# Attention in pairs: both batches of a head group are multiplied with the values in one go, and the turned probabilities go back into the probabilities' buffers

## The chip, the cores and the metric

The kernel runs on one core of a Trainium2 chip. The core has TensorE (PE in the profile: matmuls and transposes), VectorE (DVE), ScalarE (ACT), GpSimd (POOL) and SyncE (SP, which issues the transfers here); they run side by side and wait for each other by semaphores. The metric is the device time of one execution in microseconds (us); a version's time is the median of its runs.

## What is computed

One block of a transformer with cross attention, in float32. The shapes are those of the inputs: `x` and `ctx_2048` are 8 batches of 256 tokens of 512 numbers, 16 heads of 32, and an inner width of 2048. All masks are true.

```python
x = layer_norm(hidden_states, ln1_w, ln1_b)
q = (x @ q_w + q_b).reshape(B, LQ, H, HD).transpose(0, 2, 1, 3)
k = (encoder_hidden_states @ k_w + k_b).reshape(B, LK, H, HD).transpose(0, 2, 1, 3)
v = (encoder_hidden_states @ v_w + v_b).reshape(B, LK, H, HD).transpose(0, 2, 1, 3)
scores = jnp.where(mask, jnp.einsum('bhqd,bhkd->bhqk', q, k) * scale, mask_value)
attn = jax.nn.softmax(scores, axis=-1)
out = jnp.einsum('bhqk,bhkd->bhqd', attn, v)
hidden = out.transpose(0, 2, 1, 3).reshape(B, LQ, D) @ cproj_w + cproj_b + residual
y = jax.nn.gelu(layer_norm(hidden, ln2_w, ln2_b) @ fc_w + fc_b, approximate=True)
return hidden + y @ proj_w + proj_b
```

## The kernel before

**Stages.** The eight batches are four groups of two (`g` from 0 to 3; `GB` is 2). After a prologue that projects keys, queries and values of group 0 comes a long attention stage, up to 347 us of the span, and then a stage for the MLP, which this change does not touch. The projections (`project_qk`, `project_v`, `project_out`) are cut into seven products of quarters, in Strassen's way; each product is 8 or 16 matmuls in the trace and its result is taken out of its PSUM bank by DVE or ACT.

**Units.** Inside the attention stage the work is a list of 32 units `n`: group `g`, head group `hg` (four heads of 32, together 128 partitions) and batch `b` of the group. Units with even `n` have `b` = 0, units with odd `n` have `b` = 1. The main loop (line 1060) has one slot for each unit, and the order in which a slot issues its work is written by hand. On PE a slot is: the scores of unit n + 2 (`scores`, matmuls `s`, four heads side by side in the array, each with 32 rows), the transposes of the probabilities of unit n for heads 0 and 1 (`turn_probs`, tiles `ppt`), a piece or more of a projection for the next group (`between[g, u, 0]`), the transposes for heads 2 and 3, more pieces (`between[g, u, 1]`), and last the product with the values (`attend`, tile `av`, four heads side by side, each with 32 columns). Each engine runs its own instructions strictly in that order.

**The other engines in a slot.** DVE takes the scores out of PSUM (line 664: it adds the mask and finds the row's largest value), ACT takes the exponentials (line 674), DVE the reciprocals of their sums and POOL multiplies (`divide`, line 688); this runs two units ahead of the product with the values. A turned head leaves PSUM as a copy into a tile `pt` (line 702 on DVE for head 0, line 704 on ACT for heads 1 to 3). The result `av` leaves PSUM by an activation on ACT that adds the value bias (line 723).

**Buffers.** The scores of a unit fill four PSUM banks, one for each head, and the pool that holds them (`ps_s`, tag `s`) has just four. So PE can write head j of unit n + 3 only when DVE has read head j of unit n + 2. In slots 0, 1, 5 and 6 of a group the same four banks also hold context or `x` rows that are turned (`turn_ctx`, tiles `pct`; `turn_x`, tiles `pxt`; two of them in one slot), and the scores of the next slot wait until DVE and ACT have taken these out (lines 368 to 379, 415). A second pool of two banks (`ps_t`) is shared by the tiles `ppt` and `av` in turn. In SBUF the probabilities of a unit are one tile `pr` of 16 KB in each partition, with three buffers; the turned copies `pt` have four buffers of 4 KB for each partition, one for each head.

**Work beside it.** `aside[g, u, i]` holds small jobs for POOL, DVE, ACT and SP at four places of a slot: sums of weights and operands, loads and norms.

Of the kernel before, what the change touches and what calls it, by code (L numbers as in the profile page):

```python
# [10 lines left out]
F32 = mybir.dt.float32  # L11
U8 = mybir.dt.uint8
AF = mybir.ActivationFunctionType
# [3 lines left out]
P = 128  # L17
# [5 lines left out]
def tile_xattn_block(  # L23
# [45 lines left out]
    nc = tc.nc  # L69

    B, S, D = x.shape
    SK = enc.shape[1]
    INNER = fc_w.shape[1]
    HD = 32
    GB = 2
# [4 lines left out]
    NQ = S // P  # L80
    NK = SK // P
    NHG = D // P
    HPG = P // HD
    NF = INNER // P
    SCALE = 1.0 / math.sqrt(HD)
    HI, HC, HF, HD2 = INNER // 2, NC // 2, NF // 2, D // 2
# [38 lines left out]
    c_ln1w, c_ln1b, c_qb, c_kb, c_vb, c_ln2w, c_ln2b, c_fcb = col_of  # L125

    def col(base, i):
        return cols[:, base + i : base + i + 1]
# [194 lines left out]
    with ExitStack() as att:  # L323
        work = att.enter_context(tc.tile_pool(name="attwork", bufs=2))
# [3 lines left out]
        ps_t = att.enter_context(tc.tile_pool(name="ps_t", bufs=2, space=PSUM))  # L328
        ps_m = att.enter_context(tc.tile_pool(name="ps_m", bufs=1, space=PSUM))

        mbias, ctxT, xnT, vs, qk, probs, stats, res = ({} for _ in range(8))
        ctxs, xs, att_in, ws, pts = {}, {}, {}, {}, {}
# [71 lines left out]
        def turn_x(g):  # L404
            def piece(c):
                if c == 0:
                    xnT[g] = tokens_operand(work, "xT", f"xnT_{g}")
                ps = turned(f"pxt_{g}_{c}")
                turn(ps, xs[g], c)
                if g == 0 and c % 2:  # L410
                    nc.vector.tensor_scalar(
                        chunk(xnT[g], c), halves(ps), col(c_ln1w, c), col(c_ln1b, c), ALU.mult, ALU.add
                    )
                else:
                    nc.scalar.activation(
                        chunk(xnT[g], c), halves(ps), AF.Identity,
                        bias=col(c_ln1b, c), scale=col(c_ln1w, c),
                    )

            return [lambda c=c: piece(c) for c in range(NC)]  # L420
# [78 lines left out]
        def project_qk(g, tag):  # L499
            w, base = ("k", c_kb) if tag == "kT" else ("q", c_qb)  # L500

            def made(n, bank, u):
                o, k = int(n[0]) - 1, int(n[1]) - 1

                direct = g == 0 and o == 0
                st = None if direct else staged(g, tag, n)
                for i in range(2):
                    b = col(base, 2 * o + i)
                    to = qk[g, i, tag][:, ts(k, S)] if direct else st[:, i, :]
                    if u is None:  # L510
                        nc.scalar.activation(to, bank[:, i, :], AF.Identity, bias=b, scale=1.0)
                    else:
                        nc.vector.scalar_tensor_tensor(
                            to, bank[:, i, :], b, u[:, i, :], ALU.add, ALU.add
                        )
                if not direct:
                    store_quarter(g, tag, o, k, st)

            def src():
                return (ctxT if tag == "kT" else xnT)[g]  # L520

            if g == 0:
                for i in range(2):
                    qk[g, i, tag] = work.tile([P, G], F32, tag=tag, name=f"{tag}_{g}_{i}")
            if g == 0 and tag == "kT":
                return [lambda n=n: eight(f"p{tag}_{g}", n, ws[w], src, made, FIRST_KEYS.get(n, {})) for n in QUARTERS]
            return strassen(f"p{tag}_{g}", lambda: ws[w], src, False, made)
# [38 lines left out]
        def project_v(g):  # L566

            def made(n, bank, u):
                o, k = int(n[0]) - 1, int(n[1]) - 1
                st = staged(g, "v", n)  # L570
                if u is None:
                    nc.scalar.copy(st, bank)
                else:
                    nc.vector.tensor_tensor(st, bank, u, ALU.add)
                store_quarter(g, "v", o, k, st)

            return strassen(f"pv_{g}", lambda: ws["v"], lambda: ctxT[g], True, made)
# [57 lines left out]
        units = [(g, hg, b) for g in range(NG) for hg in range(NHG) for b in range(GB)]  # L635

        def scores(n):

            g, hg, b = units[n]
            qT, kT = qk[g, hg, "qT"], qk[g, hg, "kT"]  # L640
            banks = [
                ps_s.tile([P, NQ, SK], F32, tag="s", name=f"s_{n}_{j}") for j in range(HPG)
            ]
            for i in range(NQ):
                for j in range(HPG):
                    nc.tensor.matmul(  # L646
                        banks[j][:, i, :],
                        qT[j * HD : (j + 1) * HD, b * S + i * P : b * S + (i + 1) * P],
                        kT[j * HD : (j + 1) * HD, b * SK : (b + 1) * SK],
                        start=True,  # L650
                        stop=True,
                    )
            pr = work.tile([P, HPG, NQ, SK], F32, tag="pr", bufs=3, name=f"pr_{n}")
            nmax = small.tile([P, HPG, NQ], F32, tag="nmax", name=f"nmax_{n}")
            sums = small.tile([P, HPG, NQ], F32, tag="sums", name=f"sums_{n}")
            probs[n], stats[n] = pr, (banks, nmax, sums)
# [38 lines left out]
        def turn_probs(n, j):  # L695
            ps = ps_t.tile([P, NK, S], F32, tag="pt", name=f"ppt_{n}_{j}")
            for kc in range(NK):
                for i in range(NQ):
                    nc.tensor.transpose(ps[:, kc, ts(i, P)], probs[n][:, j, i, ts(kc, P)], ident)  # L699
            pt = work.tile([P, NK, S], F32, tag="pt", bufs=4, name=f"pt_{n}_{j}")  # L700
            if j == 0:
                nc.vector.tensor_copy(pt, ps)
            else:
                nc.scalar.copy(pt, ps)  # L704
            pts[n, j] = pt

        def attend(n):

            g, hg, b = units[n]
            if hg == 0 and b == 0:  # L710
                att_in[g] = Att(g)
            av = ps_t.tile([P, S], F32, tag="pt", name=f"av_{n}")
            for kc in range(NK):
                for j in range(HPG):
                    nc.tensor.matmul(  # L715
                        av[j * HD : (j + 1) * HD, :],
                        vs[g, hg][:, b * NK + kc, ts(j, HD)],
                        pts[n, j][:, kc, :],
                        start=(kc == 0),
                        stop=(kc == NK - 1),  # L720
                    )
            x, h, bias = att_in[g], hg % HC, col(c_vb, hg)
            nc.scalar.activation(
                x.t[:, hg, ts(b, S)], av, AF.Identity, bias=bias, scale=1.0
            )

        def sum_att(g, hg, eng=nc.gpsimd):
# [232 lines left out]
        g = 1  # L960
        begin(g, 6, 1, load_res, 0, *QUARTERS)
        begin(g, 7, 1, bias_res, 0)
        g = 2
# [6 lines left out]
        g = NG - 1  # L970
# [24 lines left out]
        def run(pieces):  # L995
            for p in pieces:
                p()
# [25 lines left out]
        k, q, v, tx = project_qk(0, "kT"), project_qk(0, "qT"), project_v(0), turn_x(0)  # L1023
# [19 lines left out]
        nc.gpsimd.tensor_tensor(cbd, cb[:, :S], cb[:, S:], ALU.subtract)  # L1043
        run([q[6], *normalise, v[0]])
        scores(0)
        tx = turn_x(1)
        for j, pieces in enumerate((v[1:2], v[2:3], tx[:2], v[3:4])):
# [12 lines left out]
        for n, (g, hg, b) in enumerate(units):  # L1060
            u = hg * GB + b
            ahead = n + 2 < len(units)
            if ahead:
                scores(n + 2)
                softmax(n + 2, 0)
            run(aside[g, u, 0])
            turn_probs(n, 0)
            turn_probs(n, 1)
            if n + 1 < len(units):
                divide(n + 1)  # L1070
            if ahead:
                softmax(n + 2, 1)
                softmax(n + 2, 2)
            run(between[g, u, 0])
            turn_probs(n, 2)
            turn_probs(n, 3)
            run(aside[g, u, 1])
            if ahead:
                softmax(n + 2, 3)
            run(between[g, u, 1])  # L1080
            run(aside[g, u, 2])
            attend(n)
            run(later)
            later.clear()
            run(aside[g, u, 3])
# [15 lines left out]
    with ExitStack() as mlp:  # L1101
        wpool = mlp.enter_context(tc.tile_pool(name="mlpw", bufs=1, reuse_waits="tile"))
        work = mlp.enter_context(tc.tile_pool(name="mlpwork", bufs=1, reuse_waits="tile"))
# [90 lines left out]
        for g in range(NG):  # L1194

            h = {
                n: work.tile([P, 2, HF, P], F32, tag=f"h{n}", name=f"h{n}_{g}")
                for n in ("11", "12", "21", "s3")
            }
# [413 lines left out]
```

## Time and profile before

| | |
|---|---|
| median of 3 runs | 719.96 us (719.95 to 720.17) |
| profiled execution, its own time | 719.35 us |
| its span | 717.6 us |
| PE busy | 711.9 us, 99% of the span |
| DVE, ACT, POOL busy | 71%, 46%, 66% of the span |
| attention stage | up to 347.6 us, from there the MLP |
| TensorE clock granted | 1.0 all through |

The span is from the first to the last instruction. A row of a timeline gives the start and the length in us, then engine, line of the kernel, operation, written and read tile, sizes and the number of instructions that are merged in the row; in brackets stands how long the engine sat idle before it, and which instruction ended that. In the trace each float32 matmul shows as two instructions: a tile `av` of one batch is 16 of them, in four rounds of four heads each. Ends of matmuls are modelled, so a difference of two starts on PE says more than a length.

### The profile page before, as it was taken

The page shows a single profiled execution, that of the slowest core. Times are in us where ns is not written, and L with a number is a line of the kernel's source. Part 1 is how long each engine was busy: PE and PEld are TensorE (multiplying, and loading weights), DVE is VectorE, ACT ScalarE, POOL GpSimd, SP SyncE. Part 2 cuts the span into 40 slices and gives each one's busy share as a digit, 9 for nine tenths or more (in the row PEclk, how much of TensorE's full clock was granted, in tenths as well). Part 3 has the DMA queues.
Part 4 walks back from the last instruction along what each step waited for, and adds up shares of the span by engine and source line. Part 5 has one row for each costly group of instructions (what it writes and reads, how often), then busy time and mean ns, then how long its engine had stood idle before and what let it go on. Part 6 is the DMA issues. An engine that isn't in the chain of part 4 may idle for free.

```text
span 717.6 us, 14855 instructions
## 1 busy us (share of the span) xinstructions
PE 711.9 (99%) x5397; PEld 630.3 (88%) x5397; DVE 506.7 (71%) x1212; ACT 327.7 (46%) x928; POOL 473.8 (66%) x422
## 2 busy tenths in 40 slices
PE   9999999999999999999999999999999999999998
PEld 8888777887877777777999889999999999999997
DVE  3676765674557556887678788889776897766972
ACT  2277788767866787882034400216102171030500
POOL 3858799987786999886468560792454825547253
PEclk9999999999999999999999999999999999999999
DMA  9616656597738775942699603995248942475021
GB/s 306 195 56 190 232 164 226 195 316 259 226 121 291 272 253 196 384 151 78 208 407 372 256 1 146 381 379 210 92 144 346 317 173 90 146 271 200 2 89 60
DMA packets 77545, 150.68 MB, mean 210 GB/s; under 512 B 7156, under 2 KB 45344, under 8 KB 74784
## 3 DMA queue, kind: packets, MB, share of 16 engines
q1 hardware_dynamic: 77216, 149.71, 59.4%
q8 instruction: 43, 0.70, 0.4%
q14 instruction: 30, 0.25, 0.1%
q0 software_dynamic: 256, 0.02, 0.0%
HBM read 113.01 MB, written 36.70 MB: 209 GB/s over the span
## 4 chain that ended last, share of the span: by engine, by line
PE 94%; DVE 2%; ACT 2%; POOL 1%; issue 1%; DVEq 0%; POOLq 0%
PE pf L1119 22%; PE py L1119 13%; PE ppt L699 8%; PE pv L441 7%; PE pqT L441 7%; PE po L441 6%; PE pd_t L1119 5%; PE pd L1119 5%; PE pkT L441 5%; PE s L646 5%; PE av L715 5%; PE pkT L538 2%; POOL h L1122 1%; ACT h L1259 1%; PE pxt L274 1%
## 5 line engine op out<-in xcount | busy, mean ns | idle before, releaser
L1119 PEld LDWEIGHTS pf<-y,w 128*128 128x128 f32 x1568 | 175.8, 192 | 0.3
L1119 PE MATMUL pf<-y,w 128*128 128x128 f32 x1568 | 175.9, 275 | 0.0
L1122 POOL TENSOR_TENSOR h<-h,hs 128x512 f32<-128x512 f32 x84 | 105.9, 1283 | 88.0 <-DVE hs L1122 87.8
L688 POOL TENSOR_TENSOR pr<-pr,rsum 128x512 f32<-128x512 f32 x128 | 129.5, 1045 | 36.4 <-DVE rsum L686 24.2
L674 ACT ACTIVATE pr<-pr,nmax 128x256 f32<-128x256 f32 x256 | 127.6, 501 | 35.5 <-DVE nmax L664 35.4
L664 DVE CUSTOM_DVE_ANT_0 pr<-s,mb 128x256 f32<-128x256 f32 x256 | 93.6, 413 | 39.1 <-PE s L646 27.5
L1315 ACT COPY u<-pf 128x512 f32<-128x512 f32 x28 | 16.4, 585 | 163.4 <-PE pf L1119 163.4
L699 PEld LDWEIGHTS ppt<-ident,pr 128*128 128x128 f32 x512 | 57.3, 140 | 14.9 <-issue 5.2
L699 PE MATMUL ppt<-ident,pr 128*128 128x128 f32 x512 | 68.8, 276 | 0.3
L1122 POOL TENSOR_TENSOR h<-h,h 128x512 f32<-128x512 f32 x20 | 28.8, 1463 | 52.2 <-ACT p L1452 27.1
L1122 DVE TENSOR_TENSOR hs<-pf,u 128x512 f32<-128x512 f32 x72 | 49.5, 688 | 13.1 <-PE pf L1119 11.8
L1259 ACT ACTIVATE h<-h,cols 128x256 f32<-128x256 f32 x128 | 52.0, 494 | 10.7 <-POOL h L1122 10.7
L1122 DVE TENSOR_TENSOR u<-pf,u 128x512 f32<-128x512 f32 x56 | 38.7, 691 | 25.1 <-PE pf L1119 21.1
L704 ACT COPY pt<-ppt 128x512 f32<-128x512 f32 x96 | 51.7, 573 | 7.1 <-PE ppt L699 7.1
L441 PE MATMUL pv<-vw,ctxT 128*128 128x256 f32 x224 | 52.4, 380 | 0.0
L441 PE MATMUL pqT<-xnT,qw 128*128 128x256 f32 x224 | 51.0, 379 | 0.0
L674 ACT ACTIVATION_READ_ACCUMULATOR pr<-pr,nmax 128x1 f32 x256 | 48.7, 190 | 0.0
L441 PEld LDWEIGHTS pqT<-xnT,qw 128*128 128x128 f32 x224 | 41.4, 190 | 5.0
L441 PEld LDWEIGHTS pv<-vw,ctxT 128*128 128x128 f32 x224 | 41.0, 190 | 5.4 <-issue 0.3
L1119 PE MATMUL py<-pw,h 128*128 128x256 f32 x192 | 42.4, 379 | 0.0
L1119 PE MATMUL py<-pw_t,h 128*128 128x256 f32 x192 | 42.3, 379 | 0.0
L1119 PEld LDWEIGHTS py<-pw_t,h 128*128 128x128 f32 x192 | 36.2, 190 | 4.7
(211 smaller groups left out, 1287.1 us busy)
## 6 DMA issues: line engine op xcount, KB each, us to landing
w<-w_dram SPq DMA_DIRECT2D x16, 1792.0 KB, 9.1
w<-in_L_xattn_fc_w_dram SPq DMA_DIRECT2D x36, 256.0 KB, 6.7
w<-w_dram SPq DMA_DIRECT2D x12, 768.0 KB, 7.8
p<-p_dram_t SPq DMA_DIRECT2D x6, 768.0 KB, 4.3
ctx<-in_ctx_dram SPq DMA_DIRECT2D x16, 256.0 KB, 5.0
x<-in_x_dram SPq DMA_DIRECT2D x16, 256.0 KB, 4.7
v_dram<-st_v SPq DMA_DIRECT2D x16, 256.0 KB, 2.2
v<-v_dram SPq DMA_DIRECT2D x16, 256.0 KB, 4.6
```

The source lines that it names most:

```text
L441: nc.tensor.matmul(bank[n][:, i, :], l[:, c, ts(i, P)], r[:, c, :], start=first and i == 0 and c == 0, stop=last and c == HC - 1, skip_gro ...
L646: nc.tensor.matmul(banks[j][:, i, :], qT[j * HD : (j + 1) * HD, b * S + i * P : b * S + (i + 1) * P], kT[j * HD : (j + 1) * HD, b * SK : ( ...
L664: nc.vector.tensor_tensor_reduce(pr[:, j, i, :], banks[j][:, i, :], mbias[g][1][:, b, :], scale=-SCALE, scalar=FLT_MAX, op0=ALU.add, op1=A ...
L674: nc.scalar.activation(pr[:, j, i, :], pr[:, j, i, :], AF.Exp, bias=nmax[:, j, i : i + 1], scale=-1.0, accum_out=sums[:, j, i : i + 1],)
L688: nc.gpsimd.tensor_tensor(pr[:, j], pr[:, j], rsum[:, j, :, None].to_broadcast([P, NQ, SK]), ALU.mult,)
L699: nc.tensor.transpose(ps[:, kc, ts(i, P)], probs[n][:, j, i, ts(kc, P)], ident)
L704: nc.scalar.copy(pt, ps)
L715: nc.tensor.matmul(av[j * HD : (j + 1) * HD, :], vs[g, hg][:, b * NK + kc, ts(j, HD)], pts[n, j][:, kc, :], start=(kc == 0), stop=(kc == N ...
L1119: nc.tensor.matmul(ps, lhsT, rhs, start=first, stop=last, skip_group_check=True)
L1122: eng.tensor_tensor(to, a, b, op)
L1259: nc.scalar.activation(h[n][:, :, p, :], h[n][:, :, p, :], AF.Gelu_apprx_tanh, bias=col(c_fcb, half * HF + p), scale=1.0,)
L1315: nc.scalar.copy(u1, bank[1])
```

## The change

The product with the values is no longer issued in every slot but in every second one, at the end of the slot with `b` = 1, for both batches of the head group: 32 matmuls in the trace instead of 16, into one PSUM tile of 512 columns instead of 256, and one activation of 512 columns takes it out. The turned copies of the first batch have to live one slot longer. They get no tile of their own any more: the copy of a turned head is written back into that head's part of its `pr` tile, and `pr` has four buffers instead of three. The memory in SBUF is the same: 64 KB in each partition for `pr` now, 48 KB for `pr` and 16 KB for `pt` before.

```diff
-            pr = work.tile([P, HPG, NQ, SK], F32, tag="pr", bufs=3, name=f"pr_{n}")
+            pr = work.tile([P, HPG, NQ, SK], F32, tag="pr", bufs=4, name=f"pr_{n}")
...
-            pt = work.tile([P, NK, S], F32, tag="pt", bufs=4, name=f"pt_{n}_{j}")
+
+            pt = probs[n][:, j].rearrange("p i k -> p (i k)").rearrange("p (c s) -> p c s", c=NK)
...
-            g, hg, b = units[n]
-            if hg == 0 and b == 0:
+            g, hg, _ = units[n]
+            if hg == 0:
                 att_in[g] = Att(g)
-            av = ps_t.tile([P, S], F32, tag="pt", name=f"av_{n}")
-            for kc in range(NK):
-                for j in range(HPG):
-                    nc.tensor.matmul(
-                        av[j * HD : (j + 1) * HD, :],
-                        vs[g, hg][:, b * NK + kc, ts(j, HD)],
-                        pts[n, j][:, kc, :],
-                        start=(kc == 0),
-                        stop=(kc == NK - 1),
-                    )
-            x, h, bias = att_in[g], hg % HC, col(c_vb, hg)
+            av = ps_t.tile([P, GB, S], F32, tag="pt", name=f"av_{n}")
+            for b in range(GB):
+                for kc in range(NK):
+                    for j in range(HPG):
+                        nc.tensor.matmul(
+                            av[j * HD : (j + 1) * HD, b, :],
+                            vs[g, hg][:, b * NK + kc, ts(j, HD)],
+                            pts[n - GB + 1 + b, j][:, kc, :],
+                            start=(kc == 0),
+                            stop=(kc == NK - 1),
+                        )
             nc.scalar.activation(
-                x.t[:, hg, ts(b, S)], av, AF.Identity, bias=bias, scale=1.0
+                att_in[g].t[:, hg, :].rearrange("p (b s) -> p b s", b=GB),
+                av,
+                AF.Identity,
+                bias=col(c_vb, hg),
+                scale=1.0,
             )
...
             run(aside[g, u, 2])
-            attend(n)
+            if b + 1 == GB:
+                attend(n)
```

The order of the instructions on POOL and on SP, transfers included, is the same as before. On DVE only the tile that the copy of head 0 writes is another; on ACT the 32 activations of `av` become 16.

## The prediction

> **What bounds the kernel now.** I read the page first: busy shares, then the chain that ended last.
>
> ```profile
> PE 711.9 (99%) x5397; PEld 630.3 (88%) x5397; DVE 506.7 (71%) x1212; ACT 327.7 (46%) x928; POOL 473.8 (66%) x422
> PE 94%; DVE 2%; ACT 2%; POOL 1%; issue 1%; DVEq 0%; POOLq 0%
> ```
>
> PE bounds it. What PE does not do is saved at once, unless what follows is not ready; and what follows has never been asked for earlier. So I went to the timeline: first an undisturbed slot boundary, then every place where PE, off a product with values, meets something another engine has to release.
>
> ```profile
> 254.67 1.07 PE L715 MATMUL av<-pt,v 128*32 128x256 f32 x16
> 255.67 1.15 PE L646 MATMUL s<-kT,qT 32*128 32x256 f32 x16
> 256.75 1.09 PE L699 MATMUL ppt<-ident,pr 128*128 128x128 f32 x8
> 257.68 1.89 PE L441 MATMUL pv<-vw,ctxT 128*128 128x256 f32 x8
> ```
>
> From start to start a product of one batch takes 1.00 us, scores 1.08, eight transposes 0.93. The next row is 1.73 later, at 259.41: 0.216 for a pass of 256 columns.
>
> Slot 0 (DVE row, then PE rows), slots 8 and 16:
>
> ```profile
> 59.59 1.74 DVE L379 TENSOR_TENSOR ctxT<-pct,ctxT 128x256 f32<-128x256 f32 x4 [1.96 <-ACT ctxT L369]
> 60.93 1.07 PE L715 MATMUL av<-pt,v 128*32 128x256 f32 x16
> 61.93 1.15 PE L646 MATMUL s<-kT,qT 32*128 32x256 f32 x16
> ```
>
> ```profile
> 132.44 1.74 DVE L379 TENSOR_TENSOR ctxT<-pct,ctxT 128x256 f32<-128x256 f32 x4 [2.32 <-ACT ctxT L369]
> 133.48 1.07 PE L715 MATMUL av<-pt,v 128*32 128x256 f32 x16
> 134.48 1.15 PE L646 MATMUL s<-kT,qT 32*128 32x256 f32 x16
> 216.07 1.74 DVE L379 TENSOR_TENSOR ctxT<-pct,ctxT 128x256 f32<-128x256 f32 x4 [2.27 <-ACT ctxT L369]
> 217.16 1.07 PE L715 MATMUL av<-pt,v 128*32 128x256 f32 x16
> ```
>
> The fourth bank of the next scores is the turned context that DVE reads until 61.33, 134.18 and 217.81. Scores start at 61.93, 134.48 and 218.16, after it; but `av` starts before it. The product is what PE does while DVE finishes.
>
> Slots 5 and 6:
>
> ```profile
> 107.24 1.43 ACT L415 ACTIVATE xnT<-pxt,cols 128x512 f32<-128x512 f32 x2
> 108.10 1.76 PE L646 MATMUL s<-kT,qT 32*128 32x256 f32 x16
> 115.53 1.44 ACT L415 ACTIVATE xnT<-pxt,cols 128x512 f32<-128x512 f32 x2
> 116.01 1.07 PE L715 MATMUL av<-pt,v 128*32 128x256 f32 x16
> 117.01 1.15 PE L646 MATMUL s<-kT,qT 32*128 32x256 f32 x16
> ```
>
> At 108.10 the fourth bank is late (ACT holds it to 108.67), and the scores take 1.68 to the next row at 109.78, not 1.08: a late fourth head is out of step with its three neighbours. At 51.41 the same costs 0.48 (next row 52.97). At 117.01 there is 0.04 us to spare.
>
> Slots 2 and 3:
>
> ```profile
> 80.12 1.07 PE L715 MATMUL av<-pt,v 128*32 128x256 f32 x16
> 83.34 0.69 DVE L702 COPY pt<-ppt 128x512 f32<-128x512 f32 x1
> 84.86 1.04 PE L699 MATMUL ppt<-ident,pr 128*128 128x128 f32 x8
> 86.55 0.82 ACT L511 ACTIVATE st_kT<-pkT,cols 128x256 f32<-128x256 f32 x2
> ```
>
> The copy ends at 84.03 and frees the transposes' bank at 84.86 with 0.83 to spare; ACT frees the bank of a projection at 87.37, just when PE wants it.
>
> **What the change takes from PE.** In the trace the first rounds of one product start 0.24, 0.22 and 0.22 apart; what is left of the 1.00 is the last round with the change of array shape. A second batch in the same shape adds four rounds, 4 x 0.216 = 0.865. Each pair saves 1.00 - 0.865 = 0.135, 16 pairs 2.16 us. The matmuls are the same.
>
> Second, waits of PE for evictions of `av`. The transposes at 100.58 take 1.22 to the next row (101.80) and those at 328.18 take 1.21 (to 329.39), not 0.93: the second four of them write the bank of the last `av`. Both follow an even slot and lose that wait: 0.29 + 0.28 = 0.57. Third, at 320.95 the last head's copy (ACT, line 704) is late and the product takes 1.47 (to 322.42) instead of 1.00. In the merged product the late head is in the second half, 0.865 later: 0.47. Together **-3.20 us**.
>
> **What it costs.** An even slot now ends 1.00 earlier on PE, but the work of DVE and ACT in that slot hangs on the slot's first scores, and is as late as before.
>
> - Slots 0, 8, 16: without `av` the scores would come at 60.93, 133.48, 217.16, before their fourth bank by 0.40, 0.70, 0.65. Bounds of the price of one: its lateness alone, or that plus the 0.60 of row 108.10. Up to about 0.43 (two rounds) the lateness hides behind the other heads' rounds, so I take 0.5, 0.75, 0.7, near the row 51.41: **+1.95** (1.75 to 3.55).
> - Slot 6: the fourth bank is free 8.87 after the slot's first scores (116.97 - 108.10); PE wants it after 8.91 now, 7.91 then. ACT leaves no room (busy 8.40 of the 9.0 us in this stretch). Late by 0.96; **+0.9** (0 if ACT gets ahead; 1.56 with the full price). The late head at 108.10 stays: ACT in slot 5 is busy from slot 4 on and loses one activation of `av` there (0.47), PE's scores come 0.14 and 0.29 earlier.
> - Slots 2 and 3: transposes would come 1.00 early against a copy with 0.83 to spare (0.2), those of head 3 another 0.2 (ACT's copy ends 84.67), and the projection waits for ACT's 87.37 with 0.6 of it left: **+1.0** (0 to 1.0, since the slot cannot lose more than it was moved forward).
> - The eviction of two batches. Row L723 says 474 ns for 256 columns, row L415 770 for 512, a copy of 512 takes 573 (L704). I take 770, the same operation: 0.30 longer, 0.10 at least. Scores cover it (the second transposes come 1.08 + 0.47 after the product's end) except where there are none: before 322.80, where PE waits for it already, and at the end, where DVE's sums (335.54) and then po (338.67, after 0.29 of waiting) hang on it: **+0.5** (0.2 to 0.6).
>
> The Trainium skill, "Perfetto Trace Analysis", section "Optimizing Scalar/DVE Operations", says that where ACT or DVE are not saturated but hold up other engines, smaller instructions may let work finish sooner. That speaks against the merged eviction; by it, two activations of 474 would stay and the 0.5 would be nothing.
>
> Covered, so nothing: the four `pr` buffers (the buffer for unit n + 2 was last read by the product just ahead of scores n + 2 on PE, and DVE waits for these scores anyway; price without that cover: one scores row, 1.08); the value loads (needed a slot later than now; SP's and POOL's queues keep their order); the sums of heads on POOL, which read an odd slot's result; POOL's multiplications, whose nearest margin is 0.22 us (four in 4.03 from 123.77, so head 1 is ready at 125.8, its transposes start at 126.0): by the sum above PE comes there later than before, not earlier. The other even slots end with 0.24 us or more to spare: the scores at 300.29 follow DVE's last read by 1.24, those at 315.15 by 1.66.
>
> Sum: -3.20 + 1.95 + 0.9 + 1.0 + 0.5 = **+1.15 us**. The profiled execution took 719.35 (span 717.6 and 1.75 around), which makes 720.5 of it; it is 0.61 under the median of the runs, and on the median of 719.96 the sum is **721.1 us**. A measurement of this kernel can tell about 0.2%, 1.44 us: the forecast is inside that, on the slow side.
>
> **Rivals.**
>
> - *Evictions come forward with PE, faster.* If ACT and DVE were only waiting for PE in the even slots, nothing is late and -3.20 + 0.5 = -2.7 stays: 717.3. For it: ACT's longest waits are for PE (26.4 us for `av`). Against: in slots 0, 2, 6, 8 and 16 the late row hangs on this slot's scores, and these have not moved against their own slot.
> - *A late fourth head in slots that I hold for safe, slower.* It decides once DVE's last read comes over 0.24 (scores at 300.29) or 0.66 (315.15) later in its slot. Its price is 0.5 to 0.6 each time, 1.2 for the two: 722.3. For it: the doubled eviction stands in ACT's queue ahead of the exponentials. Against: these start after PE's scores and DVE, 1.1 us later.
> - *Half of it.* The losses of slots 2, 3 and 6 turn out nil: 719.96 - 0.75 = 719.2, no change that can be told.
>
> **How the numbers follow.** Forecast case 0.62 (on its own 720.2 to 721.9), further late heads 0.18, half 0.14, all forward 0.06. The band's edge at 721.4 cuts the forecast case: about a quarter of it lies above. Slower 0.15 + 0.17 = 0.32, faster 0.06, within 0.62. Adding the lower ends of all losses to the gains gives 718.7 (-3.20 + 1.75 + 0.2), the upper ends 723.5 (-3.20 + 3.55 + 1.56 + 1.0 + 0.6). Not all go one way: 719.3 to 722.4 leaves out some two in ten.
>
> **What the profile after would show.** `av` x32 every second slot, 1.87 us to the next row; 16 rows of line 723's like near 770 ns. Scores of 1.5 us or more at the ends of slots 0, 6, 8, 16; at the other even slots the scores follow the projection at once, 1.08 long. Transposes and a projection split by waits in slot 3. No `av` of 1.47 near 321. The MLP as long as before, only shifted. Wrong it would be if scores in those four slots were 1.08, or if late heads stood in others.

## The result and the profile after

The changed kernel takes 720.98 us in the median of 22 runs (720.48 to 721.9), the kernel before, beside it on the same chip, 719.78 us (719.01 to 720.93). The ratio is 1.0017, with a 95% interval of 1.0011 to 1.0024: 1.2 us slower, inside what I had called no change that a measurement can tell, and on its slow side. The profiled execution of the changed kernel has a span of 718.9 us; before it was 717.6.

The page of the changed kernel, first the line of busy time, then that of the chain that ended last:

```profile
PE 712.3 (99%) x5397; PEld 633.1 (88%) x5397; DVE 507.6 (71%) x1212; ACT 324.8 (45%) x912; POOL 474.5 (66%) x422
PE 91%; DVE 4%; ACT 2%; issue 1%; POOL 1%; DMA 1%; SPq 0%; DVEq 0%; ACTq 0%; POOLq 0%
```

The instructions of PE are as many as before. ACT has 16 fewer and 2.9 us less work. But in the chain the share of PE falls from 94% to 91% and that of DVE rises from 2% to 4%: PE now waits for others more often. Three stages of the timeline (start and length in us) show where. First the ends of slots 0, 8 and 16: DVE's row, and the next scores on PE.

```profile
59.86 1.74 DVE L379 TENSOR_TENSOR ctxT<-pct,ctxT 128x256 f32<-128x256 f32 x4 [2.10 <-ACT ctxT L369]
61.12 1.72 PE L646 MATMUL s<-kT,qT 32*128 32x256 f32 x16
...
134.21 1.74 DVE L379 TENSOR_TENSOR ctxT<-pct,ctxT 128x256 f32<-128x256 f32 x4 [2.27 <-ACT ctxT L369]
135.30 1.90 PE L646 MATMUL s<-kT,qT 32*128 32x256 f32 x16
...
218.09 1.74 DVE L379 TENSOR_TENSOR ctxT<-pct,ctxT 128x256 f32<-128x256 f32 x4 [2.28 <-ACT ctxT L369]
219.17 1.90 PE L646 MATMUL s<-kT,qT 32*128 32x256 f32 x16
```

DVE still reads the fourth bank when the scores start, by 0.48, 0.65 and 0.66 us, and the scores take 1.65, 1.83 and 1.84 us to the next row where 1.08 is normal: 0.57 + 0.75 + 0.76 = 2.08 us lost. Slots 5 and 6:

```profile
107.24 1.93 PE L717 MATMUL av<-pr,v 128*32 128x256 f32 x32
108.13 1.45 ACT L415 ACTIVATE xnT<-pxt,cols 128x512 f32<-128x512 f32 x2
109.10 1.66 PE L646 MATMUL s<-kT,qT 32*128 32x256 f32 x16
116.50 1.44 ACT L415 ACTIVATE xnT<-pxt,cols 128x512 f32<-128x512 f32 x2
116.92 2.20 PE L646 MATMUL s<-kT,qT 32*128 32x256 f32 x16
```

The merged product stands at 107.24, with 32 matmuls; the next row starts 1.86 later. The scores at 109.10 are late in their last head as before (1.59 us to the next row). Those at 116.92 are a new case: ACT frees the bank at 117.94, and they take 2.13 us, 1.05 more than normal. Slots 2 and 3:

```profile
83.84 0.69 DVE L703 COPY pr<-ppt 128x512 f32<-128x512 f32 x1
84.68 1.33 PE L699 MATMUL ppt<-ident,pr 128*128 128x128 f32 x8
87.12 0.81 ACT L511 ACTIVATE st_kT<-pkT,cols 128x256 f32<-128x256 f32 x2
87.99 1.99 PE L441 MATMUL pkT<-ctxT,kw 128*128 128x256 f32 x8 [0.25 <-ACT st_kT L511]
```

The transposes at 84.68 start 0.19 late and take 1.16 us to the projection at 85.84, where the kernel before took 0.87 at this place, and the next projection waits at 87.99 for ACT: the two projections take 4.07 to the product instead of 3.62. Together 0.94 us. One of the gains, the transposes of slot 5 that waited for an eviction before, now 0.93 to the next row:

```profile
101.01 1.09 PE L699 MATMUL ppt<-ident,pr 128*128 128x128 f32 x8
101.94 1.89 PE L441 MATMUL pv<-vw,ctxT 128*128 128x256 f32 x8
```

Last, the eviction of two batches (count and shortest, middle and longest duration in ns), and a place where nothing covers it:

```profile
L724 ACT ACTIVATE att<-av,cols x16: 668/690/707, 72.7 to 336.4; 128x512 f32<-128x512 f32 x16
```

```profile
321.98 1.93 PE L717 MATMUL av<-pr,v 128*32 128x256 f32 x32
323.84 0.66 PE L699 MATMUL ppt<-ident,pr 128*128 128x128 f32 x4
324.81 0.63 PE L699 MATMUL ppt<-ident,pr 128*128 128x128 f32 x4 [0.31 <-ACT att L724]
```

It takes 690 ns. The second four transposes start 0.97 after the first four instead of about 0.47.

Every difference in the attention stage can be placed by the starts of the scores, since these are the same matmuls in both kernels. The start of the scores that follow a pair of slots, after minus before, moves by this much in each stretch:

| stretch | us, after minus before |
|---|---|
| prologue, ahead of any product | +0.20 |
| slots 0, 1 | +0.43 |
| slots 2, 3 | +0.80 |
| slots 4, 5 | -0.42 |
| slots 6, 7 | +0.81 |
| slots 8, 9 | +0.61 |
| slots 10 to 15 | -0.41 |
| slots 16, 17 | +0.61 |
| slots 18 to 25 | -0.41 |
| slots 26, 27 | -0.15 |
| slot 28 to the first matmul of the MLP | -0.60 |
| MLP | -0.14 |

Together +1.33. Undisturbed pairs give 0.13 to 0.15 us each, as the prediction had it (only that of slots 24 and 25 gives 0.00), and five pairs take more than all the others give.

### The profile page after: what moved, and what is told of

Its sections match the earlier page's. It is cut to its first block, busy times and chain, and to the rows that moved or that the text cites. A ratio compares the mean times of both kernels' runs of the same rounds, so it can differ in the third digit from the quotient of the medians.

```text
span 718.9 us, 14849 instructions
## 1 busy us (share of the span) xinstructions
PE 712.3 (99%) x5397; PEld 633.1 (88%) x5397; DVE 507.6 (71%) x1212; ACT 324.8 (45%) x912; POOL 474.5 (66%) x422
## 4 chain that ended last, share of the span: by engine, by line
PE 91%; DVE 4%; ACT 2%; issue 1%; POOL 1%; DMA 1%; SPq 0%; DVEq 0%; ACTq 0%; POOLq 0%
PE pf L1125 22%; PE py L1125 13%; PE ppt L699 7%; PE pv L441 7%; PE pqT L441 6%; PE po L441 6%; PE pd_t L1125 5%; PE pd L1125 5%; PE s L646 5%; PE av L717 4%; PE pkT L441 4%; PE pkT L538 2%; ACT h L1265 1%; PE pxt L274 1%; POOL h L1128 1%
## 5 line engine op out<-in xcount | busy, mean ns | idle before, releaser
L705 ACT COPY pr<-ppt 128x512 f32<-128x512 f32 x96 | 51.9, 573 | 7.6 <-PE ppt L699 7.6
L646 PE MATMUL s<-kT,qT 32*128 32x256 f32 x512 | 40.6, 403 | 0.2
```

The lines of the kernel that those rows point to most:

```text
L646: nc.tensor.matmul(banks[j][:, i, :], qT[j * HD : (j + 1) * HD, b * S + i * P : b * S + (i + 1) * P], kT[j * HD : (j + 1) * HD, b * SK : ( ...
```

## The experiments

My theory: the merged product saves 0.135 us for each pair and some waits for evictions; the losses are late readers of the scores' banks (slots 0, 6, 8, 16) and late copies (slots 2 and 3), because PE comes there 1 us earlier while DVE and ACT do not. Rivals: the new buffers and copies in place cost something themselves; the larger eviction is the loss; or the losses are general and would stay if one late reader is moved.

**One part of the change alone.** Four `pr` buffers and the copies in place, but a product for each slot (a condition in the main loop, always true here):

```diff
...
+            if n // GB in range(16):
+                attend(n, [b])
+            elif b + 1 == GB:
+                attend(n)
```

> Keeps the four probability buffers and the copies written back into them, but issues the product with the values in every slot again, one activation each. Theory (late rows in five even slots cost more than the pairing saves; the buffers cost nothing): 0.0 us against the kernel before (within 0.4), all scores 1.08 us long but those that start near 51.4 and 108.1. Rival (the shared buffers cost: probabilities stay occupied longer, copies go back into tiles that are read): about +1.2 us, as the whole change.

719.51 us; the ratio to the kernel before is 0.9993 (0.9984 to 1.0002). From slot 0 to the last scores, starts lie 0.07 to 0.18 us earlier than before, and the first scores do so by 0.08 already. The buffers and the places of the copies cost nothing that can be seen, so all that follows is the merged product.

**Merging only where nothing is late.** The same kernel with the pairs of slots 0-1, 2-3, 6-7, 8-9 and 16-17 apart, the other 11 merged:

```diff
-            if n // GB in range(16):
+            if n // GB in (0, 1, 3, 4, 8):
```

> As the changed kernel, but in the five pairs of slots 0-1, 2-3, 6-7, 8-9 and 16-17 each slot has its own product. Theory: what the other eleven pairs moved in the changed kernel's trace stays: -0.42 (slots 4-5), seven times -0.14 or so (10-15, 18-23, 26-27), 0.0 (24-25), and -0.60 from slot 28 to the MLP, together -2.0 us against before, some 717.8. Rival (each merged product costs a little everywhere, by a longer eviction and a bank held longer): eleven sixteenths of +1.2, so +0.8 us.

717.79 us, ratio 0.9971 (0.9959 to 0.9982): 2.04 us faster than before. The gain is real, and it sits where the prediction put it; what eats it are these five pairs.

**Freeing the fourth bank earlier, first try.** In the rotation's turned context, three subtractions of DVE read ACT's copy in SBUF instead of the PSUM bank:

```diff
-                        (second, x["t2"], x["t1"]),
-                        (first, x["t4"], x["t2"]),
-                        (second, x["12"], x["12"]),
+                        (x["22"][:, h, :], x["t2"], x["t1"]),
+                        (x["21"][:, h, :], x["t4"], x["t2"]),
+                        (x["22"][:, h, :], x["12"], x["12"]),
```

> As the changed kernel, but the three subtractions of the turned context read ACT's copy in SBUF, which holds the same numbers, and not the PSUM bank; so the fourth bank is free some 1.3 us earlier. Same work on every engine. Theory: the scores that end slots 0, 8 and 16 are 1.08 us again instead of 1.65, 1.83 and 1.83, so -2.1 us against the changed kernel, -0.9 against before. Rival (these scores are long because PE goes from full to quartered arrays straight from a projection, or because the second batch's work is near): they stay 1.6 to 1.8 and the time stays +1.2 against before.

The time is far from what was expected: 727.56 us, ratio 1.0106 (1.0093 to 1.012). The scores at the ends of slots 0, 8 and 16 do take 1.08 us, as expected. But slot 9 alone takes 18.18 us from scores to scores, where the changed kernel takes 11.65, a late head included. The timeline there, DVE's row, two rows of POOL, and PE's next row:

```profile
134.35 4.05 POOL L688 TENSOR_TENSOR pr<-pr,rsum 128x512 f32<-128x512 f32 x4
135.44 6.08 DVE L379 TENSOR_TENSOR ctxT<-ctxT 128x256 f32<-128x256 f32 x3
139.71 0.74 POOL L740 TENSOR_TENSOR as<-att,as 128x256 f32<-128x256 f32 x1
...
142.18 3.78 PE L441 MATMUL pqT<-xnT,qw 128*128 128x256 f32 x8 [4.02 <-DVE pqT_u L465]
```

Three subtractions that take 0.41 to 0.43 us each in the kernel before took 6.08; the longest took 5.29. It ends 0.28 us after POOL's run of instructions without a gap, which ends at 140.45. All 18 subtractions of line 379 that read two operands from SBUF (count and shortest, middle and longest duration in ns), and below them all 24 of the kernel before, which read one from PSUM:

```profile
L379 DVE TENSOR_TENSOR ctxT<-ctxT x18: 411/434/5287, 60.1 to 237.0; 128x256 f32<-128x256 f32 x18
L379 DVE TENSOR_TENSOR ctxT<-pct,ctxT x24: 411/424/426, 59.6 to 227.0; 128x256 f32<-128x256 f32 x24
```

**Is that the merged product?** The same edit in the kernel before, without anything of the change:

> The kernel before, unpaired, with only the third experiment's edit: the three subtractions of the turned context read ACT's copy in SBUF instead of PSUM. If the 8 us that the third experiment lost come from DVE instructions with both operands in SBUF waiting for a gap in POOL's run, they have nothing to do with the merged products: line 379 shows single instructions of several us here too, while POOL is busy, and the time rises by 5 us or more. Rival: they come from the merged products' new order; then the time stays within 1 us of the kernel before.

728.09 us, ratio 1.012 (1.0105 to 1.0136), so it has nothing to do with the pairs. Its timeline in slot 9, and below it the mean granted clock of TensorE in two stretches of 1 us (the number after POOL's):

```profile
133.51 4.05 POOL L688 TENSOR_TENSOR pr<-pr,rsum 128x512 f32<-128x512 f32 x4
133.78 6.90 DVE L379 TENSOR_TENSOR ctxT<-ctxT 128x256 f32<-128x256 f32 x3
138.87 0.73 POOL L735 TENSOR_TENSOR as<-att,as 128x256 f32<-128x256 f32 x1
...
141.33 3.78 PE L441 MATMUL pqT<-xnT,qw 128*128 128x256 f32 x8 [3.87 <-DVE pqT_u L465]
```

```profile
142.00:143.00 1.00, 1.00 (x4) 0.82 (x3) 1.00 (x5) 1.00 (x5) 0.16 (x1) 0.50 1.17 448
147.00:148.00 1.00, 1.00 (x9) 0.95 (x8) 0.42 (x1) 1.00 (x4) 1.00 (x1) 1.00 0.00 0
```

Here the longest took 6.10 us and ended at 139.88, again 0.28 after the end of POOL's run (139.60). The idle time is not all that it costs: PE pauses for 4.04 us (137.29 to 141.33), and then its clock stands at 0.50 until about 146.5. The eight matmuls at 141.33 take 3.57 us to the next row instead of 1.73, the transposes behind them 1.65 instead of 0.87. With 4.04 + 1.84 + 0.78 slot 9 is 6.66 us longer.

**Freeing the fourth bank earlier, in another way.** DVE takes one piece of the turned context out itself, and where ACT copies a whole bank, it does so after DVE's subtractions, which read PSUM as ever:

```diff
-                    nc.scalar.copy(x["12"][:, h, :], second)
+                    nc.vector.tensor_copy(x["12"][:, h, :], second)
...
-                    nc.scalar.copy(chunk(x, c), halves(ps))
...
                 for a, to, b in sums:
                     nc.vector.tensor_tensor(to[:, h, :], a, b[:, h, :], ALU.subtract)
+                if c >= HC:
+                    nc.scalar.copy(chunk(x, c), halves(ps))
```

> All 16 pairs stay merged; only the rotation's turned context changes: DVE copies the piece "12" from PSUM itself, and in the second half of the columns ACT's copy of the whole bank comes after DVE's three subtractions, which still read PSUM. So DVE's last read of the fourth bank no longer waits for ACT, and no subtraction has both operands outside PSUM but for those that had it before. If the late fourth heads at the ends of slots 0, 8 and 16 are what the change loses there (0.57 + 0.75 + 0.76 = 2.08 us in the changed kernel's trace), the scores there become 1.08 us and the time falls by about 2 us against the changed kernel: near 718.9, some 0.9 us below the kernel before. Rival: the lateness only moves to another reader of the bank (ACT's copy, now last), and the time stays at 721. Against the third experiment, which moved the same reads to SBUF: no DVE wait of 5 us under POOL's run, since these operations read PSUM.

718.65 us, ratio 0.9986 (0.9977 to 0.9994): 2.3 us less than the changed kernel's 720.98, by the two ratios 2.2. PE's rows at the three places, the scores and the row after them (lines are one further down here):

```profile
61.50 1.15 PE L647 MATMUL s<-kT,qT 32*128 32x256 f32 x16
62.58 0.66 PE L700 MATMUL ppt<-ident,pr 128*128 128x128 f32 x4
...
135.11 1.15 PE L647 MATMUL s<-kT,qT 32*128 32x256 f32 x16
136.19 0.98 PE L700 MATMUL ppt<-ident,pr 128*128 128x128 f32 x7
...
218.23 1.15 PE L647 MATMUL s<-kT,qT 32*128 32x256 f32 x16
219.31 1.09 PE L700 MATMUL ppt<-ident,pr 128*128 128x128 f32 x8
```

From start to start 1.08 at all three. From the first scores to the last, PE is 1.96 us faster than in the changed kernel, for 2.08 lost there; a late head at 293.32 that the changed kernel has not, of which more below, takes 0.16 of that back.

**The late head of slot 6.** The `x` rows that are turned in slots 5 and 6 of the first group leave PSUM on DVE instead of ACT, in the changed kernel:

```diff
-                if g == 0 and c % 2:
+                if g == 0 and c % 2 or g == 2:
```

> As the changed kernel, but the turned x rows of the group after next in slots 5 and 6 of group 0 that are odd or even chunks alike leave PSUM by DVE and not by ACT (four instructions of 0.77 us go from ACT to DVE). Theory: ACT's queue was what made the fourth bank late; the scores at 109.1 and 116.9 fall from 1.59 and 2.13 to 1.08, together -1.5 us against the changed kernel, -0.3 against before. Rival (DVE gets late instead, since it works ahead for the softmax): scores or transposes elsewhere in slots 5 to 7 take what is won, +1.2 stays.

719.24 us, ratio 0.9993 (0.9985 to 1.0002): 1.74 less than the changed kernel, where 1.5 was expected. By the medians it is 0.6 below the kernel before; the interval includes no difference.

```profile
108.81 1.15 PE L646 MATMUL s<-kT,qT 32*128 32x256 f32 x16
109.88 1.09 PE L699 MATMUL ppt<-ident,pr 128*128 128x128 f32 x8
...
116.11 1.15 PE L646 MATMUL s<-kT,qT 32*128 32x256 f32 x16
117.19 0.98 PE L699 MATMUL ppt<-ident,pr 128*128 128x128 f32 x7
```

Both scores are 1.08 now, the one that was late in the kernel before too.

**The late copies of slots 2 and 3.** Two pieces of the normalisation for group 2 move from slot 2 into slot 3, so that DVE has less to do ahead of the copy that was late:

```diff
-                    [(2, 1), (2, 1), (2, 2), (2, 2), (2, 2), (3, 2), (4, 1), (4, 1), (4, 2), (4, 2)],
+                    [(2, 1), (2, 1), (2, 2), (3, 1), (3, 1), (3, 2), (4, 1), (4, 1), (4, 2), (4, 2)],
```

> As the changed kernel, but two of the five small norm jobs (statistics on DVE) that stand at the third place of slot 2 stand at the second place of slot 3. Theory: they are what keeps DVE's copy of the first turned head of slot 3 (83.84 in the changed kernel's trace) behind PE; without them ahead of it the transposes, ACT's exponentials and the projection at 87.99 come sooner, and slots 2 and 3 move PE by about 0 instead of +0.80: -0.8 us against the changed kernel, +0.4 against before. Rival (ACT's own queue makes slot 3 late): the +0.80 stays, 720.9.

720.34 us, ratio 1.0004 (0.9995 to 1.0013). Slots 2 and 3:

```profile
84.74 1.04 PE L699 MATMUL ppt<-ident,pr 128*128 128x128 f32 x8
85.61 3.83 PE L441 MATMUL pkT<-ctxT,kw 128*128 128x256 f32 x16
```

The transposes take 0.87 again and no wait splits the projections, which are still 0.14 longer than in the kernel before (3.76 to the product, not 3.62). This stretch loses 0.00 us against the kernel before instead of 0.80: of the 0.94, 0.80 is back. But in slot 25 of the profiled execution stands a late head that the changed kernel has not:

```profile
293.72 0.69 DVE L244 BATCH_NORM_STATS2 st_m<-hm 128x6 f32<-128x512 f32 x1 [2.85 <-DMA hm<-hid_dram]
294.54 1.93 PE L646 MATMUL s<-kT,qT 32*128 32x256 f32 x16
```

A statistic stands on DVE ahead of a read of the scores' bank, and waits 2.85 us for its operand to be loaded. Where this wait was 0.5 us (the version with all 16 pairs, below) or 1.60 us (the changed kernel), the scores at this place took 1.08; where it was 2.09 to 2.38 (three other experiments) 1.11 to 1.57, and here, with 2.85, 1.87. Two more versions with this pair merged, with waits of 1.84 and 2.00, took 1.08. That the transfer decides it is read from these eight profiles; no run moves it. And the wait alone doesn't tell it in other orders of work: in one version of the kernel before (with subtractions from SBUF, above) 1.42 us of waiting stood beside scores of 1.36 at this place.

**Three pairs apart, the two moves with it.** Pairs of slots 0-1, 8-9 and 16-17 apart, the other 13 merged, the edits of the last two experiments:

> Products in pairs but in slots 0-1, 8-9 and 16-17, norm jobs as in the kernel with the later norm, turned x rows of slots 5 and 6 by DVE. Theory: the eleven pairs gave -2.0 us; slots 4 to 7 with DVE for the x rows are 1.17 ahead of before instead of 0.47 (from the traces of these two kernels), so 0.7 more; slots 2-3 nothing: -2.7 us against before, 717.1. Rival (the gains overlap): -2.0, 717.8.

716.98 us, ratio 0.9963 (0.9951 to 0.9975), 2.87 us faster than before.

**How much of that the moves give alone.** The two edits in the kernel before:

> The kernel before with the norm jobs and the turned x rows moved as in the best version, and nothing of the pairing. Theory: it wins only the late fourth head at 108.1 (scores 1.69 long there) and the transposes' wait at 100.6: -0.6 to -0.9 us against before. Rival (the moves are most of the best version's gain): -2 us or more.

719.36 us, ratio 0.9993 (0.9985 to 1.0002): 0.49 us by the medians, with an interval that includes no difference; in the profile it is the scores at 108.43 which are not late any more. The rest of the 2.87 is the merging.

**Two evictions instead of one.** The changed kernel, with a PSUM tile and an activation of 256 columns for each batch:

```diff
-            av = ps_t.tile([P, GB, S], F32, tag="pt", name=f"av_{n}")
             for b in range(GB):
+                av = ps_t.tile([P, S], F32, tag="pt", name=f"av_{n}_{b}")
...
-            nc.scalar.activation(
-                att_in[g].t[:, hg, :].rearrange("p (b s) -> p b s", b=GB),
...
+                nc.scalar.activation(
+                    att_in[g].t[:, hg, ts(b, S)], av, AF.Identity, bias=col(c_vb, hg), scale=1.0
+                )
```

> As the changed kernel, but the two batches' products go to two PSUM banks, each with its own activation of 256 columns. Theory: the eviction of 690 ns costs only where no scores follow; the transposes before 324.81 wait 0.2 to 0.3 us less, the end of the attention stage up to 0.2 less, nothing else moves: -0.3 us against the changed kernel, 720.7. Rival (two banks of the pool taken hold up transposes after each pair): slower, up to 0.1 or 0.2 for each of 16 pairs.

721.3 us, ratio 1.0031 (1.0018 to 1.0043): not faster, and whether slower than the change cannot be told, since the intervals overlap.

```profile
L724 ACT ACTIVATE att<-av,cols x32: 452/474/500, 74.8 to 340.2; 128x256 f32<-128x256 f32 x32
```

```profile
325.70 1.93 PE L717 MATMUL av<-pr,v 128*32 128x256 f32 x32 [0.39 <-ACT pr L705]
327.63 1.32 PE L699 MATMUL ppt<-ident,pr 128*128 128x128 f32 x8
328.79 1.89 PE L441 MATMUL po<-cw,as 128*128 128x256 f32 x8
...
334.87 0.60 PE L699 MATMUL ppt<-ident,pr 128*128 128x128 f32 x4
335.87 0.63 PE L699 MATMUL ppt<-ident,pr 128*128 128x128 f32 x4 [0.40 <-DVE pr L703]
```

The transposes that waited for the eviction take 1.16 us instead of 1.43 in the changed kernel (323.84 to 325.27). But the transposes of the last slot now take 1.46 (334.87 to 336.33) where they took 1.23, since DVE's copy is no earlier. What the shorter eviction gave (0.27), this wait took back (0.23). The profile also has two losses that are not explained by that: the merged product in front comes later (1.42 us after the row ahead of it, 1.15 in the changed kernel; it waits for ACT's copies), and the late head of slot 25 (1.57 at 298.05). So the run doesn't show what the shorter eviction is worth by itself.

**All 16 pairs.** The changed kernel with the three edits that worked: the turned context, the `x` rows, the normalisation.

> All 16 pairs merged, with the turned context's edit of the run beside it, the x rows of slots 5 and 6 by DVE, and the normalisation's pieces of group 2 one place later. If the three edits remove what each was seen to remove alone (2.08, 1.13 and 0.80 us of the changed kernel) and nothing new comes late, the time falls by about 4 us against the changed kernel, to some 716.4 to 717.0, at or below the 716.98 of the version that merges only 13 pairs. Rival: DVE, which takes work from ACT in all three, is now late for something else, and it ends above 717.5.

716.7 us, ratio 0.9957 (0.9944 to 0.9969): 2.9 us faster than before and 4.3 less than the change by the medians (4.1 if each is taken against the kernel before that was measured beside it: 719.78 to 720.98, and 719.6 to 716.7). It beats both kernels. From the version with 13 pairs it can't be told apart. Its page:

```profile
PE 708.5 (99%) x5397; PEld 631.5 (88%) x5397; DVE 510.3 (71%) x1222; ACT 320.7 (45%) x902; POOL 474.8 (66%) x422
PE 93%; DVE 2%; ACT 2%; POOL 1%; issue 1%; DVEq 0%; POOLq 0%; ACTq 0%
```

DVE's share of the chain is back to 2%, though DVE is busy 2.7 us longer than in the changed kernel: here it was not how much DVE does that mattered but what stands ahead of the reads that free a bank. The one late head of the attention stage that is left is the one at 51.30, in front of any product.

## Why the prediction was right

It forecast 721.1 us, and 720.98 came out, 1.20 above the kernel before for a sum of 1.15. By its steps:

- *Each pair saves 0.135.* Right: the undisturbed pairs moved by 0.13 to 0.15, and 11 merged pairs with the waits gained 2.04 us.
- *Waits for evictions of `av`, -0.57.* Right at 100.58: in the changed kernel the transposes there (101.01) take 0.93. The wait at 328.18 is gone too.
- *The late last head at 320.95, -0.47.* Right: the merged product at 321.98 takes the normal 1.86.
- *Slots 0, 8 and 16, +1.95.* 2.08 measured, each term 0.00 to 0.07 above mine. At these places a late fourth head cost its lateness and at most 0.1 more, so the time lay near the lower end of my bounds. One remark of the working was wrong, though the terms did not go by it: that up to about 0.43 of lateness hides behind the other heads. Nothing hid: at 51.41, before, the fourth bank came 0.44 late and cost 0.48, and at 116.83 in the first experiment it came 0.02 late and cost 0.05. That DVE's reads cause it was shown by the run that let them come earlier (1.96 us back).
- *Slot 6, +0.9.* 1.05 measured, and gone when ACT is relieved. The late head of slot 5 stayed, as I had said, but cost 0.51 instead of 0.61.
- *Slots 2 and 3, +1.0.* 0.94 (0.80 and the pair's 0.135), of which 0.80 is gone when DVE is relieved.
- *The eviction of two batches, +0.5.* Mis-sized, the one term that was: I took 770 ns from another activation of 512 columns, it takes 690, and its price at the two uncovered places is about 0.3 (0.25 at 324.81, 0.03 at the end). The rule that I weighed there (the Trainium skill, "Perfetto Trace Analysis", section "Optimizing Scalar/DVE Operations": smaller instructions may let work finish sooner where an engine that isn't saturated holds up others) holds here for that one wait and not for the time: with two activations of 474 it was 0.27 shorter, and the kernel got no faster (721.3 us), with other waits longer.
- *Not in the sum.* The transposes at 281.27 take 1.07 us, 0.14 more, for POOL's multiplications, which I had called covered. I weighed only the nearest margin, 0.22 in slot 8, where PE comes later than before; in slot 24 it was 0.33, and there, counted from the scores two slots ahead, PE comes 0.13 earlier and POOL 0.24 later. The transposes of slot 31 wait at 332.11 for DVE's copy and take 1.23 (0.88 before). And 0.20 of the profiled execution's difference arises in the prologue, where the kernels are alike. The smaller eviction and the cheaper head of slot 5 offset a good part of these, so that the sum is nearer than its terms deserve: that part is luck.
- *Rivals.* "Evictions come forward with PE, faster" is what happens in 11 pairs, and in 5 not. "A late fourth head in slots that I hold for safe" did not come in the change. Late heads did appear at the end of slot 25 in some of the other kernels, but not by what I had named, the doubled eviction in ACT's queue: there a statistic on DVE waited for its operand. "Half of it" falls, since both losses that it leaves out were measured and then removed.

## What to carry to other kernels

When work is taken from the end of a stretch on the bounding engine, look at what that engine does next and who has to release it: the removed work was also the time in which others finished, and a gain of 0.135 us for each pair turned into a loss at five places where a bank came free 0.5 to 1 us late or copies 0.2 to 0.5 us late. Such a loss isn't inherent; moving the release forward by three small edits returned 4 us here. But each released wait has to be followed to the next one, and an instruction that looks free by its busy time (the SBUF reads here) can cost more than all of it.

## What the runs showed of the hardware

**DVE behind POOL.** A DVE `tensor_tensor` of line 379 with both operands in SBUF took 0.41 to 0.44 us in 20 of 36 cases of two kernels. In 19 of the 36 cases POOL was inside an instruction when it started, and in each of them it ended about 0.28 us after the end of a POOL instruction. In 17 it was that same instruction, and DVE took up to 1.49 us; it was let in even where the next POOL instruction followed without a gap. In the other two, shown above, it waited through five and six further POOL instructions, 5.29 and 6.10 us, to the end of the whole run. Why just these two were not let in earlier stays open. With one operand in PSUM the same line took 0.41 to 0.43 us all 24 times in the kernel before, 20 of them begun while POOL was inside an instruction. The Trainium skill, "SBUF — State Buffer", section "Who interferes with whom", states that a DVE instruction with two SBUF inputs contends with a POOL instruction that reads SBUF, and that the first to issue holds the shared ports for its whole instruction while the other is blocked. The 17 cases and the 24 agree with that; two waits were far longer than one instruction.

**A pause of 4 us cost 6.7.** TensorE's granted clock is 1.0 all through before and after. In the two kernels with subtractions from SBUF it was 0.50 for 6.83 us each, from 139.65 to 146.47 in one, where PE worked again from 141.33, and from 141.49 to 148.31 in the other, where it did from 142.18. So the clock stayed low for 5.1 and 6.1 us of work, which in the first added 2.6 us to the 4.0 of the pause itself. The Trainium skill, "TensorE: Matmul & The Clock Gate", section "What's actually happening", states just two clocks, half after an idle window of about 3.4 us and full after a busy one. That fits a clock of 0.50; the way back took 5.1 and 6.1 us here, and the clock fell 2.4 and 3.5 us after the pauses had begun, the first sooner than one such window.

**A late head of four.** Four heads that run side by side take 1.08 us when all can start. When the fourth may start only 0.48, 0.65, 0.66 or 1.02 us after the others in the changed kernel, the four take 0.57, 0.75, 0.76 and 1.05 more: about the lateness and up to 0.1 on top.
